# Two graph layers on one core: places of the edges by cumulative sums over block masks instead of rank products, a deeper split of the rows, and two more FP32 chunks

## The chip, the cores and the metric

The program runs on one core of a Trainium2 chip. A core has PE (TensorE, matrix products, with its weight loads shown as PEld), DVE (VectorE), ACT (ScalarE), POOL (GpSimd, which here issues the gathers) and SP (SyncE, which here issues most plain DMAs), each with an instruction queue of its own that runs in order. The metric is the device time of one execution in microseconds (us); lower is better.

## The reference: what is computed

There are N = 20000 nodes with 256 features each and E = 340000 edges. The edges come sorted by `dst`; every node has one edge to itself, and the others stand in both directions. Each edge has one of 8 types. Cut to what matters:

```python
def rgcn(x, W, self_w, b):                       # W: 8 x 256 x 256
    msg = einsum('ni,rio->rno', x, W)[edge_type, src]
    return segment_sum(msg, dst) + x @ self_w + b

# layer 0: two relational rounds, then residual and norm
h  = relu(rgcn(x, W1, self_w1, b1))
x  = layernorm(x + rgcn(h, W2, self_w2, b2))
# layer 1: attention with 4 heads of 64; here row = src, col = dst
h  = x @ W
e  = leaky_relu(hl[src] + hr[dst])               # hl, hr: sums of a_l * h, a_r * h by head
ee = exp(e - segment_max(e, src)[src])
out = segment_sum(ee / segment_sum(ee, src)[src] * h[dst], src)
return layernorm(x + out)
```

Layer 0 sums over `dst`, in which the edges are sorted. Layer 1 sums over `src`, in which they are not; so the kernel has to put the edges into an order by blocks of 128 source nodes before it can do the attention. That ordering is what the change is about.

## The kernel before

**Sizes.** P = 128. There are NB = 157 blocks of 128 nodes. The edges stand in COLS = 2657 columns of 128. A chunk is 16 columns (2048 edges, CH); there are NC = 166 chunks.

**Three stages.** Round one and round two (`rounds`, L756) are the two relational sums, each a pass of `by_chunks` (L588) over the 2657 columns. Then comes `attention` (L1301), block by block. Each stage gathers one 128-row tile per column with an indirect DMA from POOL: L607 in the rounds, L1354 in attention.

**A column in `by_chunks`.** POOL gathers 128 rows of the table at the columns' sources, AHEAD = 23 columns ahead, into one of 24 buffers `g`. PE multiplies them with a one-hot of destination and type (L727; the one-hots are made by DVE at L630, two of 1216 elements a chunk, or at L620 where rows are FP32) into PSUM tiles `a`. ACT and DVE evacuate these twice a chunk (L652, L650; the L650 copy closes a chunk), DVE adds the part carried over from the chunk before (L739), and `make` (L654) multiplies by the weights of the types (L662 to L674). `use` finishes the rows: in round one relu and a split in three BF16 parts (ACT L850, L854; DVE L852, L856), stored to the table `h2s` that round two gathers from.

**Rows as three BF16 parts.** The tables `xs` and `h2s` hold each row as three BF16 parts, so that PE can work in BF16 without losing FP32's digits. `xs` has to be made first: `split_rows` (L286) loads blocks of x, subtracts BF16 parts (ACT L301, L305; DVE L307, L312) and stores them with SP. Until then the first RAW = 26 chunks gather the FP32 rows of x themselves. When the gather of the first later chunk is put into the program, what is left of `split_rows` is drained before it (L603 to L605).

**Order by hand.** The pools' releases and the order of all instructions are as written (`manual_schedule`, L760): beside the chunks' own work, `by_chunks` takes side steps from a generator, at most one per column (L743): `pace(u)` says in which columns. In round one the side steps are the preparation of the edges (`heads`), then `split_rows` (two steps a block), then `order` (L795); round two goes on with `order`. In round one a step is taken in every column up to column 2 NB + COLS/3 + 120 and in five of six after that (L861); in round two in five of eight (L915).

**The ordering, class `ordered` (L918).** The columns are dealt to G = 29 groups: group g has the columns g, g + 29, and so on. `lots` are three columns of a group each. The steps:
- `count` (L994): a compare makes, for each lot, the one-hots of the block of each edge, `b16` (128 x 3 x 157; DVE L965), and one product a column (L1006) counts the edges by block.
- `records` (L970): seven passes of DVE over all 2657 columns pack what an edge has to carry into `hi` and `lo`.
- `places` (L1014): from the counts by group, where each group's edges of a block begin, within a record of 128 places; this also yields the list of the record rows.
- `write` (L1090): for each lot again the one-hots (L965), the rank of each edge among those of its block by two products a column (L1120, L1121), the place by a product with the one-hots and a maximum along the row (DVE L1141, L1144, L1145), a one-hot of the place `a16` (L1147), the one-hots scaled by `hi` and `lo` (`two`; ACT L1131, L1132, two a column), and one product a column (L1159) that sums a group's edges into records; `finish` (L1166) stores them. PSUM tiles `pr` and `pl` are used by all of this, one buffer each; `pending` keeps `use` off `pr` while a rank stands in it.
- `unpack` (L1255): after the rounds, 23 gathers (L1262) bring the records back in the order of blocks.

Of the kernel before, what the change touches and what calls it, by code (L numbers as in the profile page):

```python
# [34 lines left out]
F32 = mybir.dt.float32  # L35
# [12 lines left out]
P = 128  # L48
# [17 lines left out]
AHEAD = 23  # L66
# [8 lines left out]
def gnn_kernel(  # L75
# [39 lines left out]
    RAW = min(26, NC // 2)  # L115
# [11 lines left out]
    GT = min(P, NB * 19 // 32)  # L127
    G = -(-COLS // GT)
# [157 lines left out]
    def split_rows(sp):  # L286

        def load(i):
            v = sp.tile([P, D], F32, name="y", bufs=4)
            nc.sync.dma_start(v[:rows(i)], x[i * P:i * P + rows(i)])  # L290
            return v
# [4 lines left out]
        for i in range(NB + 1):  # L296
# [13 lines left out]
            if i < NB:  # L310
                left = sp.tile([P, D], F32, name="x1")
                nc.vector.tensor_sub(left[:m], v[:m], t[:m, 0])  # L312
                old = m, i, left, t
# [69 lines left out]
    def edges(k, keep, pool, ps, words):  # L383


        NQ = -(-COLS // P)
# [48 lines left out]
        k["kb"] = keep.tile([P, COLS], FP16, name="kb")  # L435
        k["idx"], k["code"] = [], []
# [16 lines left out]

        for s, (q, n) in enumerate(slices):
# [8 lines left out]
            k["idx"].append(idx)  # L463
            fs = number(fs, n, nc.vector.tensor_copy)
# [31 lines left out]
            if s + 1 < len(slices):  # L496
                x_, n_ = slices[s + 1]
                got[s + 1] = [flat(src, x_, n_, -P, nc.sync), flat(dst, x_, n_, -NP, nc.sync),
                              flat(etype, x_, n_, 0, nc.sync)]
# [18 lines left out]
            yield  # L518
            v = m * T
# [24 lines left out]
            if s + 1 < len(slices):  # L544
                got[s + 1].append(flat(dst, x_, n_, NP, nc.sync, 1))
# [3 lines left out]
            cl = pool.tile([P, CS], BF16, name="cl")  # L549
            yield from turned(same, q, n, cl)  # L550
            block = pool.tile([P, CS], F32, name="at").bitcast(I32)
            nc.vector.tensor_single_scalar(block[:, :w], lo, 7, op=ALU.arith_shift_right)
            nc.vector.scalar_tensor_tensor(k["kb"][:, c:c + w], cl[:, :w], 1024.0, block[:, :w],
                                           op0=ALU.mult, op1=ALU.add)
# [201 lines left out]
    def rounds(words):  # L756
        with tc.tile_pool(name="pi", bufs=1, space=PSUM) as cps, tc.tile_pool(name="rows", bufs=1) as keep, \
# [7 lines left out]
            pi = cps.tile([P, WIDE], F32, name="pi")  # L765
            nc.vector.tensor_copy(pi, wide_iota)
# [4 lines left out]
            parts = split_rows(sp)  # L771
# [23 lines left out]
    def order(ranks, ps, pi, words):  # L795
        with tc.tile_pool(name="order", bufs=2) as op:
            yield from ranks.run(op, ps, pi)
        ranks.over = True
        yield
        with tc.tile_pool(name="unpack", bufs=2) as up:  # L800
            yield from ranks.unpack(up, ps, *words)
# [23 lines left out]
    def round_one(k, pools, wp, first, parts, side, ranks):  # L825
# [21 lines left out]
        def use(j, p, _):  # L847
# [13 lines left out]
                  lambda u: u < 2 * NB + COLS // LOT + 120 or u % 6, False, ranks, RAW, parts)  # L861

    def round_two(k, pools, wp, side, ranks):
# [51 lines left out]
        by_chunks(h2s, AHEAD, k, pools, weights, load, use, side, lambda u: u % 8 < 5, True, ranks)  # L915


    class ordered:  # L918
# [6 lines left out]
        def __init__(self, keep, k):  # L925
# [8 lines left out]
            self.count_all = keep.tile([P, G, NB], FP16, name="count_all")  # L934
# [3 lines left out]
            self.band = keep.tile([P, 2 * P - 1], FP16, name="band")  # L938
            nc.vector.memset(self.band, 0.0)
            nc.vector.memset(self.band[:, P - 1:P], 1.0)  # L940
# [4 lines left out]
            self.below16 = keep.tile([P, P], FP16, name="below16")  # L945
            nc.vector.tensor_copy(self.below16, self.below)
# [10 lines left out]
            for g in range(G):  # L957
                n = len(range(g, COLS, G))
                self.lots += [(g, i, min(LOT, n - i), n) for i in range(0, n, LOT)]

        def blocks_of(self, sp, pi, lot):
            g, i, n, _ = lot
            b = sp.tile([P, LOT, NB], FP16, name="b16", bufs=4)
            c = g + G * i
            nc.vector.tensor_tensor(b[:, :n], pi[:, :NB].unsqueeze(1).to_broadcast([P, n, NB]),  # L965
                                    self.k["kb"][:, c:c + G * (n - 1) + 1:G].unsqueeze(2).to_broadcast([P, n, NB]),
# [21 lines left out]
        def run(self, sp, ps, pi):  # L988
            yield from self.count(sp, ps, pi)
            yield from self.records()  # L990
            yield from self.places(sp, ps)
            yield from self.write(sp, ps, pi)

        def count(self, sp, ps, pi):  # L994

            made = {m: self.blocks_of(sp, pi, self.lots[m]) for m in range(2)}
            pc, done = None, 0
            for m, (g, i, n, of) in enumerate(self.lots):
                if m + 2 < len(self.lots):
                    made[m + 2] = self.blocks_of(sp, pi, self.lots[m + 2])  # L1000
                b = made.pop(m)
                for x in range(n):
                    u = i + x
                    if u == 0:
                        pc = ps.tile([P, 512], F32, name=("pr", "pl")[g % 2])[:, :NB]
                    nc.tensor.matmul(pc, self.band[:, P - 1 - u:2 * P - 1 - u], b[:, x, :],  # L1006
                                     start=(u == 0), stop=(u == of - 1))
                    if u == of - 1:
                        nc.scalar.copy(self.count_all[:, g, :], pc)
                    done += 1  # L1010
                    if done % LOT == 0:
                        yield

        def places(self, sp, ps):  # L1014
# [3 lines left out]
            for g in range(G):  # L1018
                nc.tensor.matmul(pc, self.band[:, P - 1 - g:2 * P - 1 - g], self.count_all[:, g, :],
                                 start=(g == 0), stop=(g == G - 1))  # L1020
# [69 lines left out]
        def write(self, sp, ps, pi):  # L1090
# [7 lines left out]
            def begin(g):  # L1098


                x = ps.tile([P, 512], F32, name="pr")[:, :3 * NB].rearrange("p (a b) -> p a b", a=3)
                nc.tensor.matmul(x[:, 0, :], self.below16, self.count_all[:, g, :], start=True, stop=False)
                of = self.ident16[:, g:g + 1].to_broadcast([P, P])
                nc.tensor.matmul(x[:, 0, :], of, self.place16, start=False, stop=True)
                nc.tensor.matmul(x[:, 1, :], of, self.place16, start=True, stop=True)
                nc.tensor.matmul(x[:, 2, :], of, self.cross16, start=True, stop=True)
                start = sp.tile([P, NB], FP16, name="start")
                nc.scalar.copy(start, x[:, 0, :])
                cross = sp.tile([P, NB], F32, name="cross")
                nc.scalar.copy(cross, x[:, 2, :])  # L1110
                mine = sp.tile([P, NB], F32, name="mine")
                nc.vector.tensor_scalar(mine, x[:, 1, :], self.row, None, op0=ALU.is_le)
                group[g] = start, cross, mine

            def rank(m):
                g, i, n, _ = lots[m]
                pr = ps.tile([P, 512], F32, name="pr")[:, :LOT * NB].rearrange("p (x b) -> p x b", x=LOT)
                self.pending = True
                for x in range(n):
                    nc.tensor.matmul(pr[:, x, :], self.below16, made[m][:, x, :], start=True, stop=False)  # L1120
                    nc.tensor.matmul(pr[:, x, :], self.ident16[:, i + x:i + x + 1].to_broadcast([P, P]), group[g][0],  # L1121
                                     start=False, stop=True)
                ranked[m] = pr
# [806 lines left out]
```

## Time and profile before

| | |
|---|---|
| median of three runs | 10266.15 us (10256.0 to 10272.33) |
| profiled execution, its own time | 10269.47 us |
| its span | 10267.7 us |
| busy: PE, PEld | 8999.7 us (88%), 6985.1 us (68%) |
| busy: DVE, ACT | 7476.9 us (73%), 5836.7 us (57%) |
| busy: POOL | 7646.4 us (74%) |
| gathers from x and xs, from h2s, from table3s | 2657, 2657, 2657 |
| first gather of xs starts at | 607.39 us |
| first gather of h2s (round two) at | 3458.35 us |
| first gather for attention at | 6848.11 us |

How to read it: busy times are sums over the span, and stages differ. So the stretches matter more than the totals; POOL's busy time is the 0.95 us of each gather and leaves out what lies between two of them. In lists of instructions `out<-in` are the program's tile names with partitions x elements, `[0.30 <-PE a L727]` is the idle time before an instruction and what ended it. Line numbers are those of the kernel before.

### The profile page before, as it was taken

What the parts mean: (1) busy time and instruction counts of PE and PEld (TensorE: products, weight loads), DVE (VectorE), ACT (ScalarE), POOL (GpSimd) and SP (SyncE); (2) the same over time, 40 slices, a digit from 0 to 9 for tenths busy, and PEclk for the clock granted to TensorE, in tenths of its full rate; (3) what the DMA queues carried; (4) which work ended last, traced back from release to release, by engine and by line L of the source; (5) the groups of instructions that cost most, each with busy time, mean ns of one, the idle gap of its engine ahead of it and who ended that gap; (6) DMA issues with size and microseconds to landing.
All of it is one profiled execution on the core that took longest, in us unless ns stands there. A gap on an engine that the chain in (4) does not pass through costs nothing. (4 is left out here: it accounts for less than half of the span.)

```text
span 10267.7 us, 220891 instructions
## 1 busy us (share of the span) xinstructions
PE 8999.7 (88%) x75895; PEld 6985.1 (68%) x75895; DVE 7476.9 (73%) x21331; ACT 5836.7 (57%) x18175; POOL 7646.4 (74%) x8041
## 2 busy tenths in 40 slices
PE   7889999999999899999999999977777777777777
PEld 6778888888888788888888888854444444444444
DVE  5466667777777666666666666548888888888888
ACT  2321112555555544444444444438888888888888
POOL 7767777777777677777777777777777777777776
PEclk9999999999999999999999999989999999999999
DMA  5766666666666566666666666655555555555554
GB/s 176 233 185 179 179 178 174 179 179 177 179 178 178 171 188 189 187 187 189 186 188 187 184 186 185 186 164 156 154 154 153 155 154 154 155 154 153 155 155 129
DMA packets 860800, 1779.85 MB, mean 173 GB/s; under 512 B 196893, under 2 KB 525835, under 8 KB 859643
## 3 DMA queue, kind: packets, MB, share of 16 engines
q0 software_dynamic: 461712, 1386.83, 49.2%
q1 hardware_dynamic: 390098, 371.58, 11.6%
q8 instruction: 597, 9.78, 0.4%
q10 hardware_dynamic: 7848, 7.20, 0.2%
q14 instruction: 545, 4.46, 0.2%
HBM read 1632.08 MB, written 132.98 MB: 172 GB/s over the span
## 5 line engine op out<-in xcount | busy, mean ns | idle before, releaser
L1354 POOL DMA_INDIRECT g<-table3s,words x2657 | 2564.3, 965 | 812.7 <-issue 771.7
L607 POOL DMA_INDIRECT g<-h2s,idx x2657 | 2518.5, 948 | 873.2 <-issue 369.1
L674 PE MATMUL pm<-wt,to 128*128 128x256 f32 x10624 | 2894.5, 395 | 0.0
L727 PE MATMUL a<-s,g 128*128 128x152 bf16 (+8 forms) x34932 | 2793.8, 223 | 54.8 <-ACT xs L301 16.0
L607 POOL DMA_INDIRECT g<-xs,idx x2241 | 2134.2, 952 | 710.8 <-issue 277.8
L727 PEld LDWEIGHTS <-g 128*128 128x128 bf16 x33060 | 2127.5, 98 | 312.2 <-DMA g<-xs,idx 23.2
L1456 ACT ACTIVATE g<-g 128x64 f32<-128x64 f32 x8088 | 1993.0, 332 | 0.0
L674 PEld LDWEIGHTS pm<-wt,to 128*128 128x128 f32 x10624 | 1814.8, 191 | 179.7 <-issue 2.5
L1470 PE MATMUL po<-g,s 128*128 128x260 f32 x5314 | 1739.0, 418 | 106.4 <-DVE g L1462 78.8
L652 ACT COPY to<-a 128x512 f32<-128x512 f32 x996 | 546.3, 583 | 1948.9 <-PE a L727 1920.0
L1414 DVE CUSTOM_DVE_ANT_0 dump<-pr,pen 128x768 bf16<-128x768 f32 x1876 | 1621.5, 908 | 33.1 <-PE pr L1411 31.4
L1411 PE MATMUL pr<-hpt,pick 128*128 128x512 bf16 (+2 forms) x3752 | 937.3, 333 | 421.3 <-DVE top L1414 419.5
L1141 DVE CUSTOM_DVE_ANT_0 dump<-pr,b 128x157 f16<-128x157 f32 x2657 | 712.4, 320 | 777.8 <-PE pr L1121 768.0
L1131 ACT ACTIVATE two<-b,words 128x157 f16<-128x157 f16 x2657 | 1123.4, 423 | 182.3 <-DVE b L965 119.4
L965 DVE TENSOR_TENSOR b<-pi,kb 128x471 f16<-128x471 f32 (+1 forms) x1798 | 1104.5, 635 | 144.5 <-PE pr L1006 73.6
L1470 PEld LDWEIGHTS po<-g,s 128*128 128x128 f32 x5314 | 850.6, 197 | 467.7 <-ACT g L1447 83.6
L1132 ACT ACTIVATE two<-b,words 128x157 f16<-128x157 f16 x2657 | 1102.5, 415 | 0.0
L1411 PEld LDWEIGHTS <-pick 128*128 128x128 bf16 x3752 | 379.2, 101 | 920.0 <-issue 794.0
L630 DVE TENSOR_TENSOR s<-pi,code 128x1216 bf16<-128x1216 f32 (+1 forms) x614 | 866.8, 1412 | 0.0
L1159 PE MATMUL pl<-two,a 128*128 128x314 f16 x2657 | 508.0, 300 | 50.1 <-DVE a L1147 48.4
L1400 ACT CAST hpt<-pr 12x768 bf16<-12x768 f32 (+1 forms) x469 | 350.0, 747 | 341.2 <-PE pr L1398 341.1
L739 DVE TENSOR_TENSOR to<-to,to 128x192 f32<-128x192 f32 x330 | 119.0, 361 | 582.5 <-ACT to L652 582.2
(290 smaller groups left out, 10582.4 us busy)
## 6 DMA issues: line engine op xcount, KB each, us to landing
ob<-ownd SPq DMA_DIRECT2D x625, 128.0 KB
g<-h2s,idx POOLq DMA_INDIRECT x2657
g<-table3s,words POOLq DMA_INDIRECT x2657
y<-in_x SPq DMA_DIRECT2D x321, 128.0 KB
g<-xs,idx POOLq DMA_INDIRECT x2241
h2s<-h SPq DMA_DIRECT2D x166, 192.0 KB
own<-h2s SPq DMA_DIRECT2D x166, 192.0 KB
xs<-xs SPq DMA_DIRECT2D x156, 192.0 KB
```

Of the source, the lines that this page charges most:

```text
L607: nc.gpsimd.indirect_dma_start(out=g, out_offset=None, in_=of, in_offset=bass.IndirectOffsetOnAxis(ap=idx[u // CS][:, u % CS:u % CS + 1], ...
L630: nc.vector.tensor_tensor(s, pi[:, :w].unsqueeze(1).to_broadcast([P, e - f, w]), codes(c, e - f).unsqueeze(2).to_broadcast([P, e - f, w]), ...
L674: nc.tensor.matmul(p, to[:, i % 2, i // 2, :P], wt[:, i % 2, i // 2, :], start=False, stop=(i == 2 * R - 1))
L727: nc.tensor.matmul(a[h, q][:, b:e, :].rearrange("p n r -> p (n r)"), g[:, v * D + h * P:v * D + (h + 1) * P], s, start=((h, q) not in begu ...
L965: nc.vector.tensor_tensor(b[:, :n], pi[:, :NB].unsqueeze(1).to_broadcast([P, n, NB]), self.k["kb"][:, c:c + G * (n - 1) + 1:G].unsqueeze(2 ...
L1131: nc.scalar.activation(two[:, 0, :], made[m][:, x, :], AF.Copy, scale=k["hi"][:, c:c + 1])
L1132: nc.scalar.activation(two[:, 1, :], made[m][:, x, :], AF.Copy, scale=k["lo"][:, c:c + 1])
L1354: nc.gpsimd.indirect_dma_start(out=g[:, t, :], out_offset=None, in_=table3s, in_offset=bass.IndirectOffsetOnAxis(ap=to3[:, b, t:t + 1], ax ...
L1411: nc.tensor.matmul(pr[:, t:t + n, :], pick[:, h, :], k["hpt"][:, q + t:q + t + n, :], start=True, stop=True)
L1414: nc.vector.tensor_tensor_reduce(out=dump[:, :m, :].rearrange("p t e -> p (t e)"), in0=pr[:, :m, :].rearrange("p t e -> p (t e)"), in1=k[" ...
L1456: nc.scalar.activation(gh[:, h, :], gh[:, h, :], AF.Copy, scale=k["g"][:, t, D + h:D + h + 1])
L1470: nc.tensor.matmul(k["po"], k["s"][:, t, :] if t < n else ident, k["g"][:, t, :SR], start=(t == 0), stop=(t == n))
```

## The change

What it does, in four parts:
1. `split_rows` opens a pool of its own with four buffers for each tile (five for the loaded rows) instead of sharing the rounds' pool with two; RAW is 28 instead of 26.
2. The groups are made otherwise: column c belongs to row r = c mod 128, and a group is RG = 4 such rows, so G = 32. The block numbers of the edges are kept in a second layout, `kbflat` (128 x 21 x 128, BF16): partition r holds the edges of the columns r, r + 128, and so on, one after the other. `edges` builds it directly from the loaded sources (`block`, `to`) and turns it into `kb`; the loads of the second slice move behind the code of the first.
3. `count` and the ranking in `write` are gone. `rank` comes in their place: for each of the 157 blocks ACT makes a 0/1 mask of 2688 elements a partition in two passes (Square, then Relu, which also sums it); PE multiplies the sum with `below` (a product of one column); DVE makes a running sum over the mask in PSUM, started from that, in six pieces of at most 512, and after each a predicated copy puts it into `place` where the mask is 1. Each block has eleven steps. At the end three DVE passes over all places take them modulo 128, and PE and ACT turn them into `slots`.
4. `write` has two steps a lot instead of three, without the rank products and the reductions; the one-hot of the place compares with `slots`. In round one a side step is taken in every column, in round two in five of nine.

The core of the diff:

```diff
-    RAW = min(26, NC // 2)
+    RAW = min(28, NC // 2)
...
-    GT = min(P, NB * 19 // 32)
-    G = -(-COLS // GT)
+    RG = 4
+    G = P // RG
+    NQ = -(-COLS // P)
...
-    def split_rows(sp):
+    def split_rows():
+        with tc.tile_pool(name="split", bufs=4) as sp:
+            yield from split_in(sp)
...
-            v = sp.tile([P, D], F32, name="y", bufs=4)
+            v = sp.tile([P, D], F32, name="v", bufs=5)
...
-            cl = pool.tile([P, CS], BF16, name="cl")
-            yield from turned(same, q, n, cl)
-            block = pool.tile([P, CS], F32, name="at").bitcast(I32)
-            nc.vector.tensor_single_scalar(block[:, :w], lo, 7, op=ALU.arith_shift_right)
-            nc.vector.scalar_tensor_tensor(k["kb"][:, c:c + w], cl[:, :w], 1024.0, block[:, :w],
-                                           op0=ALU.mult, op1=ALU.add)
+            to = k["flat"][:, q:q + n]
+            nc.vector.scalar_tensor_tensor(to, same[:, :n], 1024.0, block[:, :n], op0=ALU.mult, op1=ALU.add)
+            yield from turned(to, q, n, k["kb"][:, c:c + w])
...
-            pi = cps.tile([P, WIDE], F32, name="pi")
+            pi = cps.tile([P, WIDE + 1], F32, name="pi")
...
+        with tc.tile_pool(name="rank", bufs=2) as op:
+            yield from ranks.rank(op, ps, pi[:, WIDE:])
...
-                  lambda u: u < 2 * NB + COLS // LOT + 120 or u % 6, False, ranks, RAW, parts)
+                  lambda u: True, False, ranks, RAW, parts)
...
-        by_chunks(h2s, AHEAD, k, pools, weights, load, use, side, lambda u: u % 8 < 5, True, ranks)
+        by_chunks(h2s, AHEAD, k, pools, weights, load, use, side, lambda u: u % 9 < 5, True, ranks)
...
+            for b in range(NB):
+                mask = sp.tile([P, NQ * P], BF16, name="mask")
+                nc.scalar.activation(mask, every, AF.Square, bias=wide_iota[:, b:b + 1], scale=-1.0)
+                yield
+                nc.scalar.activation(mask, mask, AF.Relu, bias=ones[:, 0:1], scale=-1.0,
+                                     accum_out=self.hist[:, b:b + 1])
+                yield
+                pb = ps.tile([P, 512], F32, name="pr")
+                nc.tensor.matmul(pb[:, 0:1], self.below, self.hist[:, b:b + 1], start=True, stop=True)
+                yield
+                nc.vector.tensor_single_scalar(less[:, b:b + 1], pb[:, 0:1], -1.0, op=ALU.add)
+                yield
+                at, old = less[:, b:b + 1], None
+                for i, (c, n) in enumerate(cuts):
+                    scan = ps.tile([P, 512], F32, name=("pl", "pr")[i % 2])[:, :n]
+                    nc.vector.tensor_tensor_scan(scan, mask[:, c:c + n], zero.to_broadcast([P, n]), at,
+                                                 op0=ALU.add, op1=ALU.add)
+                    at = scan[:, n - 1:n]
+                    if old:
+                        nc.vector.copy_predicated(*old)
+                    old = place[:, c:c + n], mask[:, c:c + n].bitcast(I16), scan
+                    yield
+                nc.vector.copy_predicated(*old)
+                yield
+            slots = flat.rearrange("p q r -> p (q r)").bitcast(FP16)[:, :COLS]
+            whole = sp.tile([P, NQ * P], F32, name="whole", bufs=1).bitcast(I32)
+            nc.vector.tensor_copy(whole, place)
+            yield
+            nc.vector.tensor_single_scalar(whole, whole, P - 1, op=ALU.bitwise_and)
+            yield
+            nc.vector.tensor_copy(place, whole)
...
             def place_of(m):
...
-                    nc.vector.tensor_tensor_reduce(out=dump, in0=pr[:, x, :], in1=made[m][:, x, :], scale=1.0,
-                                                   scalar=0.0, op0=ALU.mult, op1=ALU.max, accum_out=r[:, x:x + 1])
...
-                                        r[:, :n].unsqueeze(2).to_broadcast([P, n, P]), op=ALU.is_equal)
+                                        self.slots[:, c:c + P * (n - 1) + 1:P].unsqueeze(2).to_broadcast([P, n, P]),
+                                        op=ALU.is_equal)
...
-                    rank(m + 1)
                     place_of(m + 1)
```

## Prediction

> **What bounds the kernel now.** First I read the table of busy time in stretches of 200 us (columns: stretch, length, then busy us and instruction count of PE, PEld, VectorE, ScalarE, POOL, then granted clock, DMA share, GB/s):
>
> ```profile
> 200.00:400.00 200.00, 170.18 (x1028) 152.91 (x1027) 98.36 (x219) 77.67 (x200) 139.73 (x146) 0.96 0.77 231
> 1000.00:1200.00 200.00, 193.81 (x2020) 167.86 (x2019) 137.28 (x224) 30.07 (x67) 151.44 (x160) 1.00 0.62 178
> 4000.00:4200.00 200.00, 188.49 (x1849) 161.73 (x1849) 130.48 (x467) 96.95 (x279) 151.26 (x161) 1.00 0.67 188
> 8000.00:8200.00 200.00, 155.81 (x876) 89.79 (x875) 177.11 (x437) 170.67 (x582) 151.88 (x159) 0.96 0.57 155
> ```
>
> Look at POOL's count: about 160 gathers per 200 us in round one, round two and attention alike, though PE, VectorE and ScalarE are loaded quite differently. Only the first row (FP32 chunks) has fewer. The timeline of POOL says why, and where the exceptions are:
>
> ```profile
> 1203.94 0.94 POOL L607 DMA_INDIRECT g<-xs,idx  x1 [0.30 <-PE a L727]
> 1205.19 0.95 POOL L607 DMA_INDIRECT g<-xs,idx  x1 [0.30 <-PE pl L1006]
> ...
> 578.03 0.94 POOL L607 DMA_INDIRECT g<-in_x,idx  x1 [0.52 <-PE a L727]
> 607.39 1.10 POOL L607 DMA_INDIRECT g<-xs,idx  x1 [28.42 <-PE a L727]
> ...
> 3423.03 0.95 POOL L607 DMA_INDIRECT g<-xs,idx  x1 [0.30 <-issue]
> 3458.35 0.94 POOL L607 DMA_INDIRECT g<-h2s,idx  x1 [34.37 <-PE pl L1159]
> ```
>
> A gather takes 0.95 us and is followed by 0.30 us of idleness whatever the releaser named: one per 1.25 us. The page counts 3 x 2657 of them, and the unpacking adds 23: 7994 x 1.25 = 9993 us of the 10267.7 us span. The kernel is **bound by POOL issuing gathers**, and a change can win only what POOL waits beyond 0.30 us. Adding that up over POOL's timeline: 45 us before 580, 28.1 before the first gather of xs, 34.1 between the rounds, 29.6 between 4500 and 6600, 3.3 before attention: 140 us. Another 83 us are gathers longer than 0.95 us, 50 of them in attention, which is untouched.
>
> Next, how far PE is behind POOL: VectorE's L650 copy closes a chunk of 16 tiles; I take its start less the end of that chunk's last gather. It is 32 to 35 us in the FP32 chunks of the row splitting (chunk 16: 413.9 against 381.8), falls 0.45 us a chunk through the counting, is 5 us at chunk 107, 19.6 at the end of round one, 25 to 30 through the second half of round two, and falls 3 us a chunk once the writing is over there (6618.5, 6635.9, 6653.2: 17.2 us a chunk where POOL needs 20). With 24 gather buffers (30 us) POOL feels PE only where this distance is near 26 or more: in the FP32 chunks and in round two. So PE work removed elsewhere gives nothing by itself.
>
> **The change part by part** (against the profiled execution's 10269.5 us; the median shown is 3.3 us less).
>
> *Row splitting.* The waits between 200 and 560 (engine, line, what it waited for: us, times, longest):
>
> ```profile
> ACT xs L305 <- DMA xs<-xs: 136.8, 104, 2.9
> DVE x L312 <- ACT xs L305: 136.7, 113, 2.9
> PE pm L670 <- ACT ot L665: 37.7, 16, 3.7
> PE a L727 <- ACT xs L301: 16.0, 10, 2.3
> ```
>
> ScalarE stops 1.3 us a row for the store of the row before last, VectorE stops behind it, and PE then waits 53.7 of 360 us for copies queued behind that stop. The store waited for was issued one step (two tiles, 2.75 us) earlier, so it takes some 4.1 us; four buffers leave three steps, 7.5 us: the wait goes. A chunk here takes 22.0 us (288 gathers from 182.3 to 578.0: 1.374 us each), of which PE idles 53.7/360 x 22.0 = 3.3; 18.7 remain, under POOL's 20. So POOL is next, at 1.25: 288 x 0.124 = 35.7 us less. Then the 28.1 us: in the built program the first xs gather is placed at tile 416 - 23 = 393, when 13 rows are unsplit and are drained at once (L305 runs last at 603.1, the gather starts at 607.4). With 28 chunks it is placed at 425, and the splitting ends at 420, 6 us earlier, against 4.1 us of store. I leave 3 us of that gap. The two further FP32 chunks stay under POOL's pace (18.7 against 20). Sum: **-61**; bounds -64 (all) and 0 (the cover of the distance gone, the gap merely moved).
>
> *Counting becomes ranking*: 157 blocks of 11 steps, one step a tile, 13.75 us a block at POOL's pace. Removed: 2657 matmuls and 886 compares, hidden behind POOL: nothing. Added, per block:
> - ScalarE: two passes over 2688 elements. From L652 (512 wide: 0.58) and L665 (256 wide: 0.36), 2.5 us each, 5 us; its present work in round one is 30 of 200 us, 2.1 a block. 7.1 of 13.75: hidden.
> - PE: one matmul of one column. At 17.2 us a chunk, PE needs 11.8 us for 11 tiles: 1.9 us spare.
> - VectorE: six scans and six predicated copies (five of 512, one of 128). Neither is in the trace. Steps between starts, read where two instructions follow closely:
>
> ```profile
> 3422.90 1.41 DVE L630 TENSOR_TENSOR s<-pi,code 128x1216 bf16<-128x1216 f32 x1
> 3424.23 0.64 DVE L965 TENSOR_TENSOR b<-pi,kb 128x471 f16<-128x471 f32 x1
> ...
> 3442.28 0.68 DVE L650 COPY to<-a 128x512 f32<-128x512 f32 x1
> 3442.88 0.64 DVE L965 TENSOR_TENSOR b<-pi,kb 128x471 f16<-128x471 f32 x1
> ```
>
>   1216 elements: 1.33; 512: 0.60; so 1.04 ns an element, and 0.20 for 128. Lower bound 0.60, upper bound 1.33, for scan and copy each. VectorE's present work per chunk: 2 x 1.33 + 0.60 + 0.28 (L739) + 0.34 (L852) + 0.33 (L856) + 0.28 of idleness before L739 = 4.5, so 3.1 for 11 tiles. A block with both at 0.60: 5 x 1.20 + 0.40 + 0.35 (the small add and waits) + 3.1 = 9.9 us. Scan at 1.33: 13.5. Both at 1.33: 17.2. I take 0.60 for both, by L650, which has their width and reads PSUM; the first two sums stay under 13.75, so the forecast needs only the copy to be ordinary. **0**; bounds 0 and +534 ((17.2 - 13.75) x 157), of which the gathers ahead absorb some 25.
>
> [...] No run here shows a scan yet. [...]
>
> *Three passes over all places* (to integers, mask, back). The like passes of the records (L973 to L984, seven of them) stretch five gathers at 1697.8 to 1710.3 by 7.1 us together; three more: **+3** (0 to +7).
>
> *Writing.* Per lot of three columns the rank matmuls and reductions go; blocks, `two`, the transposed one-hots and three matmuls stay, in two steps. ScalarE's `two` starts every 0.32 us: 6 x 0.32 = 1.9 us a lot of 2.5 us in round one, plus 0.3 of its other work: 88%. PE: three matmuls step by 0.41 together (3439.54 to 3439.95), 8 lots a chunk: 3.3 us. The counting shows PE at 19.55 us a chunk with 48 matmuls of 0.067 in it: 16.3 without. 19.6 of 20. The distance should stay low: 8 us at the end of round one rather than 19.6, and the gap of 34 us shrinks by **-11** (0 to -15; 16 us of it are the last chunk's own chain). In round two, 16 x 5/9 / 2 = 4.4 lots a chunk: 17.2 + 4.4 x 0.41 = 19.0 of 20, so the distance falls instead of standing at 26, and the 29.6 us go: **-29** (0 to -30).
>
> Sum: -61 + 0 + 3 - 11 - 29 = **-98**: 10269.5 - 98 = 10171.5, some 10168 beside the median; I say **10170**. With the three waits gone as far as their bounds allow it would be 10160.
>
> **Rivals.**
> *A. VectorE becomes the bound* (the one that ends slower). The next block's small matmul on PE waits for the last predicated copy of this block, for their shared PSUM tile `pr`, and everything behind it on PE, the chunks' matmuls, waits too. From 1.98 us per 512-wide scan plus copy the block passes 13.75 us; each 0.1 us more costs 5 x 0.1 x 157 = 79 us; from 2.14 it eats the gain. At both upper bounds: 10171 + 534 - 25 = 10680; midway 10400. For it: neither price is known. Against: it needs both near the price of 1216 elements.
> *B. Not the throughput but the loop.* ScalarE's sum for a block stands one step before that matmul; if a pass sits behind an evacuation that waits for PE, PE waits for up to 5 us less three steps. A period of 14.2 instead of 13.75: 0.45 x 157 - 25 = +46: 10215. PE's spare 1.9 us speak against, VectorE's queue (scans between evacuations) for.
> *C. The FP32 stretch stays slow*, held by its transfers: the DMA engines are 77% busy at 1.374 us a gather and would be 85% at 1.25. Then only the 28 us go: 10207.
> *D. The change does not do what it says*: the distance at the end of round one stays, ScalarE at 88% in order being the late one: 10182, within the forecast's own range.
>
> **How the numbers follow.** Forecast with D 54% (10145 to 10190; its low end is that 10160 less the 16 us over which the runs shown spread), B 20% (10190 to 10250), C 10% (near 10207), A 16% (from 10250 up). The range 10145 to 10290 takes in the first three and the beginning of A. A measurement here tells about 0.2% (20 us) from no change. Faster: 54 + 10 + 17 of B = 81%; within: 3 of B and 3 of A = 6%; slower: 13%.
>
> **What would show it.** Right: POOL at 160 gathers per 200 us from 200 on; no gap over 5 us at the first xs gather; L305's wait for its store gone; VectorE 65 to 95% busy between about 550 and 2700, with the L650 distance falling there; a gap near 23 us between the rounds; none in round two. Wrong: under 158 gathers per 200 us in the ranking, with PE waiting for VectorE or ScalarE at the small matmul; scan plus copy over 1.98 us; POOL's gathers stretched beyond 0.95 us by the new VectorE work, which like L630 and L965 reads one operand from PSUM and which I therefore count at nothing.

## The result: slower by 4%, and where the time went

| | before | after |
|---|---|---|
| median of four runs each | 10268.83 us (10256.0 to 10272.33) | 10685.3 us (10681.54 to 10688.19) |
| ratio, 95% interval | | 1.0408 (1.039 to 1.0426) |
| profiled execution, its span | 10267.7 us | 10679.8 us |

10170 had been predicted, with 10145 to 10290 as the range. Lines of the kernel after carry other numbers than before: the gather is L618 (was L607), the copy that closes a chunk L661 (L650), a column's product L738 (L727). New are ACT's two passes L1016 and L1018, the one-column product L1022, DVE's running sum L1029 and its predicated copies L1033 and L1036.

POOL's gathers come in the same order in both kernels, so a gather's start in the one less its start in the other tells how much had been lost up to there:

| up to | after less before | of that in this stage | predicted |
|---|---|---|---|
| column 416 of round one, before's first gather of xs (splitting) | -55.0 us | -55 | -61 |
| column 2200 of round one (ranking, then whole passes and records) | +369.4 | **+424** | 0 and +3 |
| last column of round one (writing) | +408.4 | +39 | -11, with the next line |
| first gather of round two | +423.0 | +15 | |
| first gather for attention | +405.6 | -17 | -29 |
| end of the span | +412.1 | +7 | 0 |

The ranking alone loses as much as the whole kernel, and the splitting won nearly what was forecast. The busy time by stretches of the two kernels, before first (columns: stretch, its length, PE, PEld, DVE, ACT and POOL busy with their instructions, PE's granted clock, DMA share, GB/s):

```profile
200.00:400.00 200.00, 170.18 (x1028) 152.91 (x1027) 98.36 (x219) 77.67 (x200) 139.73 (x146) 0.96 0.77 231
800.00:1000.00 200.00, 192.71 (x2022) 167.13 (x2019) 138.24 (x224) 30.05 (x67) 151.27 (x161) 1.00 0.63 178
2000.00:2200.00 200.00, 189.08 (x1898) 160.04 (x1896) 145.53 (x512) 113.40 (x334) 151.52 (x160) 1.00 0.63 179
```

The same stretches of the kernel after:

```profile
200.00:400.00 200.00, 191.23 (x1192) 170.51 (x1192) 114.60 (x265) 89.79 (x242) 152.41 (x157) 1.00 0.85 266
800.00:1000.00 200.00, 154.31 (x1273) 129.75 (x1273) 158.18 (x205) 82.84 (x85) 123.82 (x132) 0.84 0.51 147
2000.00:2200.00 200.00, 152.22 (x1240) 128.63 (x1238) 159.53 (x207) 84.16 (x85) 125.80 (x133) 0.84 0.52 149
```

POOL's count is the pace. In the splitting it rises from 146 to 157 gathers per 200 us. In the ranking it falls from 160 to 132, and there **no engine is full**: between 800 and 1000 PE is 77% busy, DVE 79%, ACT 41%. What sets the pace is then not one engine's work but the waits between engines. POOL's timeline in the kernel after shows the places that had been looked at before:

```profile
552.35 0.95 POOL L618 DMA_INDIRECT g<-in_x,idx  x1 [0.30 <-issue]
...
592.85 0.95 POOL L618 DMA_INDIRECT g<-xs,idx  x1 [0.30 <-issue]
...
1446.02 0.95 POOL L618 DMA_INDIRECT g<-xs,idx  x1 [0.31 <-issue]
1450.55 0.95 POOL L618 DMA_INDIRECT g<-xs,idx  x1 [3.58 <-PE a L738]
...
3831.40 0.95 POOL L618 DMA_INDIRECT g<-xs,idx  x1 [0.42 <-PE a L738]
3881.31 0.95 POOL L618 DMA_INDIRECT g<-h2s,idx  x1 [48.96 <-PE pl L1178]
```

Before's 28.4 us of idleness ahead of column 416 are gone: the kernel after, with 28 FP32 chunks, still gathers from x there, at 552.35, and its first gather of xs, 32 columns later, follows its forerunner after 0.30 us. In the ranking POOL now waits up to several us at a time for PE. And the gap between the rounds grew from 34.4 to 49.0 us. What PE waits for between 800 and 2800 (engine, line, what it waited for: us, times, longest):

```profile
PE pr L1022 <- ACT mask L1018: 215.3, 53, 5.9
PE pr L1022 <- DVE place L1036: 154.9, 55, 6.5
PE pm L685 <- DVE to L661: 67.7, 17, 5.2
PE pr L1022 <- DVE to L661: 34.6, 7, 5.1
```

The busy time of these 2000 us, with the columns as above:

```profile
800.00:2800.00 2000.00, 1531.79 (x12790) 1291.98 (x12791) 1589.81 (x2065) 833.58 (x860) 1258.30 (x1327) 0.84 0.51 148
```

POOL issued 1327 gathers, so 120.6 blocks of eleven, each of 16.6 us instead of 13.8 (11 x 1.253, POOL's pace where nothing holds it: in the kernel before 639 gathers from 799.33 to 1598.75). PE was busy for 1531.8 us, 12.7 a block; it stood 3.4 us a block at the little product L1022 and 0.6 at L685: together 16.6, rounding aside, the whole block. One such ring, in the timeline of the kernel after:

```profile
1441.13 1.29 DVE L1029 TENSOR_TENSOR_SCAN pl<-mask,pr,pi 128x512 f32<-128x512 bf16 x1
1441.33 1.72 PE L738 MATMUL a<-s,g 128*128 128x144 bf16 x24
1441.53 0.39 ACT L866 ACTIVATE h<-pm 128x256 bf16<-128x256 f32 x1 [2.65 <-PE pm L685]
1442.34 0.72 DVE L1033 COPY_PREDICATED place<-mask,pr 128x512 f32<-128x512 int16 x1
1442.95 0.41 DVE L868 SCALAR_TENSOR_TENSOR left<-pm,h 128x256 f32<-128x256 f32 x1
...
1443.39 0.41 ACT L870 CAST h<-left 128x256 bf16<-128x256 f32 x1 [1.48 <-DVE left L868]
...
1443.71 2.53 ACT L1016 ACTIVATE mask<-kbflat,wide_iota 128x2688 bf16<-128x2688 bf16 x1
...
1446.27 2.54 ACT L1018 ACTIVATE mask<-mask,ones 128x2688 bf16<-128x2688 bf16 x1
1448.71 0.19 ACT L1018 ACTIVATION_READ_ACCUMULATOR mask<-mask,ones 128x1 f32 x1
1448.95 0.58 PE L1022 MATMUL pr<-hist,below 128*128 128x1 f32 x2 [5.90 <-ACT mask L1018]
```

ACT waits 2.65 us for PE's L685 and 1.48 for DVE's L868, which itself stands behind the scan and the predicated copy shown above it; only then do its two passes start, though the first of them reads neither result, and PE, having run out of work at 1443.05, waits for their end. Each engine has room, but each waits in its turn for another one's queue.

### The profile page after: what moved, and what is told of

The parts are those of the page before. It is cut to its first block, busy times and chain, and to the rows that moved or that the text cites. A ratio compares the mean times of both kernels' runs of the same rounds, so it can differ in the third digit from the quotient of the medians.

```text
span 10679.8 us, 199248 instructions
## 1 busy us (share of the span) xinstructions
PE 8845.1 (83%) x68106; PEld 6702.8 (63%) x68106; DVE 7499.6 (70%) x15385; ACT 6573.9 (62%) x18606; POOL 7671.9 (72%) x8044
## 4 chain that ended last, share of the span: by engine, by line
PE 42%; DVE 21%; ACT 14%; issue 9%; POOL 9%; DMA 4%; SPq 0%; ACTq 0%; DVEq 0%; POOLq 0%
PE pm L685 20%; PE a L738 12%; POOL g L1361 8%; DVE dump L1421 5%; PE pm L681 3%; DVE place L1033 3%; DVE pl L1029 2%; ACT g L1463 2%; DVE pr L1029 2%; PE pl L1178 2%; ACT two L1158 2%; ACT two L1159 2%; DMA g<-table3s,words 2%; ACT mask L1018 1%; PE pr L922 1%
## 5 line engine op out<-in xcount | busy, mean ns | idle before, releaser
L618 POOL DMA_INDIRECT g<-h2s,idx x2657 | 2525.3, 950 | 863.5 <-issue 375.9
L685 PE MATMUL pm<-wt,to 128*128 128x256 f32 x10624 | 2999.3, 406 | 88.3 <-DVE to L661 88.3
L738 PE MATMUL a<-s,g 128*128 128x152 bf16 (+9 forms) x34860 | 2913.0, 230 | 66.5 <-DMA g<-h2s,idx 31.2
L618 POOL DMA_INDIRECT g<-xs,idx x2209 | 2106.5, 954 | 1133.3 <-PE a L738 784.9
L738 PEld LDWEIGHTS <-g 128*128 128x128 bf16 x32844 | 2291.1, 102 | 486.2 <-issue 77.2
L685 PEld LDWEIGHTS pm<-wt,to 128*128 128x128 f32 x10624 | 1870.4, 197 | 292.0 <-DVE to L661 99.3
L641 DVE TENSOR_TENSOR s<-pi,code 128x1216 bf16<-128x1216 f32 x610 | 859.5, 1409 | 0.0
L1178 PE MATMUL pl<-two,a 128*128 128x314 f16 x2657 | 554.3, 302 | 126.7 <-DVE a L1165 75.9
L982 DVE TENSOR_TENSOR b<-pi,kb 128x471 f16<-128x471 f32 (+1 forms) x896 | 568.2, 634 | 1.3 <-ACT two L1159 1.3
L618 POOL DMA_INDIRECT g<-in_x,idx x448 | 443.9, 991 | 144.1 <-issue 75.0
```

The costliest lines, as they stand in the source:

```text
L618: nc.gpsimd.indirect_dma_start(out=g, out_offset=None, in_=of, in_offset=bass.IndirectOffsetOnAxis(ap=idx[u // CS][:, u % CS:u % CS + 1], ...
L641: nc.vector.tensor_tensor(s, pi[:, :w].unsqueeze(1).to_broadcast([P, e - f, w]), codes(c, e - f).unsqueeze(2).to_broadcast([P, e - f, w]), ...
L685: nc.tensor.matmul(p, to[:, i % 2, i // 2, :P], wt[:, i % 2, i // 2, :], start=False, stop=(i == 2 * R - 1))
L738: nc.tensor.matmul(a[h, q][:, b:e, :].rearrange("p n r -> p (n r)"), g[:, v * D + h * P:v * D + (h + 1) * P], s, start=((h, q) not in begu ...
L1178: nc.tensor.matmul(pl[0].rearrange("p a b -> p (a b)"), a[:, x, :], ranked.pop((m, x)).rearrange("p a b -> p (a b)"), start=(first and x = ...
```

## The experiments

Two theories. **Loop** (theory 1 in the expectations): PE stands at L1022 because ACT's sum and DVE's last copy of the block before come late in their queues; moving these away from the product cures it. **VectorE** (theory 2): a scan with its copy takes too long for eleven steps; only less work or more steps help. Times in the ranking are given for a block, from POOL's gathers between 800 and 2800. e2, e3, e6, f2 and g3 are one execution each; runs of one kernel spread over some 16 us.

**ACT's passes a block ahead (e2).** The two passes for block b + 1 are issued among the scans of block b; the block keeps eleven steps.

```diff
-                nc.scalar.activation(mask, every, AF.Square, ...)     # and Relu, each before a yield
+                mask = masks.pop(b)
...
+                    if b + 1 < NB and i == 1:
+                        squares(b + 1)
+                    if b + 1 < NB and i == 3:
+                        ones_of(b + 1)
...
+                yield
+                yield
```

> The changed kernel, with ScalarE's two passes for the next block put among this block's scans (eleven steps a block still), so that their sum is there long before PE's one-column product. Theory 1 (a loop: PE stands at that product, 3.4 us a block, 236 of 449 us for ScalarE and 173 for the last predicated copy): the ScalarE part goes, about 1.8 us of each of 157 blocks, so 10400 to 10450 instead of 10685; PE's idle time before the product falls to the copy's share. Theory 2 (VectorE is simply too slow: scan plus copy 1.96 us a cut): nothing changes, 10660 to 10690.

10387.8 us, 298 less than the kernel after and 12 below the range of theory 1; theory 2 had it unchanged. PE's waits between 800 and 2800 in this kernel, where the product is L1031 and the last copy L1049:

```profile
PE pr L1031 <- DVE place L1049: 213.6, 104, 5.3
PE pm L681 <- ACT ot L676: 145.2, 51, 3.8
```

The wait for ACT's sum is gone and the block takes 14.7 us instead of 16.6; 0.9 over POOL's pace remain, now with DVE named at the product and ACT at L681.

**The product in a place of its own (e3), and both (e4).** The one-column product writes a spare column of the tile `pi` instead of `pr`, so that DVE's last copy out of `pr` needn't be over.

```diff
-                pb = ps.tile([P, 512], F32, name="pr")
-                nc.tensor.matmul(pb[:, 0:1], self.below, ...)
+                pb = zero[:, 1:2]                                     # pi is one column wider
+                nc.tensor.matmul(pb, self.below, ...)
```

> The changed kernel, with the one-column product written to a free column beside the constants in PSUM instead of the tile pr that the scans use, so that it no longer waits for the last predicated copy. Theory 1 (loop): the wait for VectorE (173 us in 133 blocks, 1.3 us a block) goes, the one for ScalarE stays: 10480 to 10600. Theory 2 (VectorE too slow): 10660 to 10690, since the scans themselves are as long.

> Both edits together: passes one block ahead, and a PSUM column of its own. Theory 1 (loop): the ranking goes at POOL's pace, 13.8 us a block for 16.55; VectorE's 13.2 us of work still fit. The 424 us lost between gathers 480 and 2200 come back but for some 50: 10260 to 10320. Theory 2 (VectorE too slow): 10600 or more.

e3: 10681.7 us, no change. e4: 10390.4 us (four runs, ratio to before 1.0123, 1.0106 to 1.014), no better than e2 and in neither theory's range. PE's waits in e3 tell why:

```profile
PE pi L1022 <- ACT mask L1018: 214.0, 52, 5.9
PE pi L1022 <- DVE s L641: 186.3, 39, 7.8
```

The edit exchanged the wait for L1036 for one of the same size: DVE's L641 reads the same tile `pi`, and it is in the same queue. So e3 did not take the wait for DVE away. That its time lies in theory 2's range therefore says little; what e3 shows is that the product waits for DVE's *queue*, whichever of its instructions it is that it needs.

**Five of six predicated copies left out (e6).** The places are not made, so the edges' records and attention's lists of rows are not those of the reference.

```diff
-                    if old:
-                        nc.vector.copy_predicated(*old)
```

> The changed kernel without five of the six predicated copies of a block (only the last, of 128 places, is left; the places of the others stay zero, so the order of the edges is not made). VectorE has 3.3 us less to do in a block, 9.9 instead of 13.2. Theory 2 (VectorE too slow): POOL's pace, 10250 to 10290. Theory 1 (loop): PE's wait for VectorE goes, that for ScalarE stays or grows: 10450 to 10550.

11772.6 us, which neither theory foresaw. The trace puts the surplus behind the ranking: up to the first attention gather e6 is 261 us ahead of the kernel after (6992.9 against 7253.7), and then loses some 1350 in attention, whose gathers by these lists are slow (last section). So only the ranking is read: 14.95 us a block. PE's waits there:

```profile
PE pr L1022 <- ACT mask L1018: 318.8, 82, 5.3
PE pm L685 <- DVE to L661: 35.9, 17, 2.7
PE pr L1022 <- DVE place L1034: 11.0, 9, 1.3
```

DVE is now 68% busy (1365.5 of 2000 us) and PE's wait for its last copy is nearly gone, but the wait for ACT's sum is larger than in the kernel after. Each theory has half: taking either engine out of the way leaves 0.9 to 1.2 us a block.

**Both out of the way, and more steps instead of less work.** Two readings of what e2 still loses, V and P, stand in the expectations below. Four kernels: row splitting alone (e1, read below); passes ahead and five copies left out (e8); passes ahead and 13 steps a block (e9) or 12 (e10), by two idle `yield`s or one at the end of a block and a pace in round two of 5 in 8 or 3 in 5, since the writing starts later.

```diff
-                  lambda u: u % 9 < 5, True, ranks)
+                  lambda u: u % 8 < 5, True, ranks)
...
                 nc.vector.copy_predicated(*old)
                 yield
                 yield
                 yield
+                yield
+                yield
```

> The kernel before with the first part of the change alone: row splitting with four buffers of its own and 28 FP32 chunks; the ranking by matrix products stays. If the 55 us that the changed kernel was ahead at its first gather of xs are this part's, and are kept to the end because nothing after them has changed: 10205 to 10225 us. If they are given back at the end of round one or in round two, where the distance between POOL and PE is largest, 10255 to 10270.

> The kernel with ScalarE's two passes moved a block ahead, and five of the six predicated copies of a block left out as well, so that the places are not made and nodes get wrong slots; the attention stage then fetches the same rows again and again, so only the time up to the first attention gather is read (6848 us before, 7254 after, 6968 with the passes ahead alone). Theory V, that what is left of the loss in the ranking is VectorE's queue (13.0 us of work in a block of 13.75): the ranking runs at 157 to 160 gathers per 200 us and the first attention gather comes at 6790 to 6830. Theory P, that PE alone, at the granted clock of 0.89 it has there, takes 1.33 us a tile: 150 gathers per 200 us and 6950 to 6970, as with the passes ahead alone.

> The passes ahead, and 13 steps to a block in place of 11 (16.25 us at POOL's pace); the writing then begins 317 tiles later and runs in round two at 5 steps of 8 in place of 5 of 9. Theory V: VectorE has 13.6 us of work in 16.25 us, the ranking runs at 158 to 160 gathers per 200 us, the distance falls in it and the gap between the rounds is near 30 us: 10205 to 10250 us. Theory P: 150 gathers per 200 us over more tiles, 10380 to 10430.

> The same with 12 steps to a block (15.0 us at POOL's pace) and 3 steps of 5 in round two. Theory V: VectorE has 13.3 us of work in 15.0; the ranking runs at 155 to 160 gathers per 200 us: 10210 to 10300 us. Theory P: 150 gathers per 200 us, 10380 to 10420.

Beside these four the kernel before itself took 14124.57 us (e1 14080.05, e8 13829.57, e9 13870.04, e10 13811.71 us; ratios to before 0.9967, 0.9954 to 0.9979, for e1 and 0.9813, 0.9797 to 0.983, for e9). Why all of them took so long was not tried; they can't be set beside the runs above, and the kernels were run again beside a kernel before of some 10270 us.

> The passes ahead, 13 steps to a block (16.25 us at POOL's pace), 5 steps of 8 in round two; the same kernel as e9, beside a kernel before of some 10267 us. Theory V (VectorE's queue, 13.6 us of work in 16.25): 158 to 160 gathers per 200 us in the ranking, 10205 to 10250 us. Theory P (PE alone needs 1.33 us a tile at the granted clock of 0.89): 150 gathers per 200 us, 10380 to 10430.

> The passes ahead, and five of the six predicated copies of a block left out; the places are not made, so only the time up to the first attention gather is read (6848 us before, 7254 after, 6968 with the passes ahead alone). Theory V: 157 to 160 gathers per 200 us in the ranking, first attention gather at 6790 to 6830. Theory P: 150 per 200 us, 6950 to 6970.

f1: 10259.2 us (ratio 0.9996, 0.9986 to 1.0005), 9 over the range of theory V. f2: first attention gather at 6815.7 us, as theory V had it. The ranking in f1, by stretches as above:

```profile
800.00:1000.00 200.00, 173.39 (x1531) 143.09 (x1530) 165.27 (x216) 87.40 (x98) 151.26 (x161) 0.91 0.62 178
1800.00:2000.00 200.00, 171.13 (x1530) 140.54 (x1528) 171.53 (x226) 88.69 (x99) 151.55 (x160) 0.93 0.62 178
```

And in f2, from 800 to 2600 in one:

```profile
800.00:2600.00 1800.00, 1547.18 (x13836) 1278.44 (x13834) 1324.60 (x1582) 896.83 (x929) 1362.35 (x1438) 0.92 0.63 178
```

160 gathers per 200 us in both: POOL is the bound again, and the ranking is as theory V had it; what f1 loses beyond that lies after it, at the gap between the rounds (47.4 us) and in round two. f2 reaches POOL's pace with eleven steps at a granted clock of 0.92. In e2, at 0.89, PE was not the bound either:

```profile
800.00:2800.00 2000.00, 1641.20 (x14377) 1368.66 (x14375) 1787.68 (x2327) 930.00 (x965) 1420.68 (x1498) 0.89 0.58 167
```

1641 us for 1498 tiles are 1.10 us a tile, not 1.33: theory P falls.

**Is more slack alone enough, and how much is needed?** g3 is the kernel after with 13 steps and 5 in 8, ACT's passes left in place; g2 is e10 again.

> The changed kernel with 13 steps to a block and 5 of 8 in round two, but ScalarE's two passes left where they are, a step and two ahead of the small product. If slack for VectorE is the whole cure: 158 to 160 gathers per 200 us in the ranking and 10245 to 10275 us, as with the passes ahead and 13 steps (10259). If the order of the loop costs by itself, PE standing at the small product for ScalarE's sum whatever the budget: PE's waits there stay near 1.5 to 2 us a block and the ranking at 135 to 152 gathers per 200 us, 10350 to 10600.

> The passes ahead, 12 steps to a block (15.0 us at POOL's pace) and 3 steps of 5 in round two, as in e10. If VectorE's work alone counts (13.3 us of 15.0, 89%): 158 to 160 gathers per 200 us in the ranking, as with 13 steps, and less distance to pay for in round two than 5 of 8 cost (the first 30 us): 10225 to 10255 us. If waits of the loop still come on top at 89%: 152 to 157 gathers per 200 us and 10270 to 10350.

g3: 10493.73 us, 17.7 us a block of 13, 1.4 over POOL's pace. Its PE waits between 800 and 2800:

```profile
PE pr L1022 <- ACT mask L1018: 287.9, 71, 5.3
PE pm L685 <- DVE to L661: 129.6, 35, 5.2
PE pr L1022 <- DVE place L1036: 6.8, 14, 0.5
```

The wait for DVE's last copy has gone with the slack, the one for ACT has not (2.5 us a block), and the one at L685 has grown. g3 and f1 differ only in where ACT's passes stand, so the order costs by itself. g2: 10250.53 us (ratio 0.9977, 0.9967 to 0.9986), as expected if VectorE's work alone counts; its ranking and PE's longest wait for another engine there:

```profile
800.00:2800.00 2000.00, 1714.35 (x15337) 1408.12 (x15336) 1782.47 (x2324) 927.16 (x996) 1513.88 (x1595) 0.93 0.62 178
```

```profile
PE pr L1031 <- DVE place L1049: 50.5, 36, 2.1
```

With DVE busy 13.4 of 15.0 us the ranking costs nothing. All variants of the ranking together; the budget is the steps times 1.253, times are for a block:

| kernel | ACT's passes | budget | DVE busy | block | over the budget |
|---|---|---|---|---|---|
| after | in place | 13.8 us | 13.2 us | 16.6 us | 2.8 us |
| e3, own column | in place | 13.8 | 13.2 | 16.7 | 2.9 |
| e6, five copies out | in place | 13.8 | 10.2 | 14.95 | 1.2 |
| g3, 13 steps | in place | 16.3 | 13.8 | 17.7 | 1.4 |
| e2 | a block ahead | 13.8 | 13.1 | 14.7 | 0.9 |
| e4, own column | a block ahead | 13.8 | 13.1 | 14.8 | 1.0 |
| f2, five copies out | a block ahead | 13.8 | 10.1 | 13.8 | 0 |
| g2, 12 steps | a block ahead | 15.0 | 13.4 | 15.05 | 0 |
| f1, 13 steps | a block ahead | 16.3 | 13.7 | 16.3 | 0 |

With DVE at 74% of the budget (e6) or 85% (g3) ACT in place costs 1.2 to 1.4 us a block. A DVE at 95% costs 0.9 with ACT's passes ahead (e2), and the two together 2.8, more than their sum.

**Row splitting alone (g1).** The kernel before, with only part 1 of the change.

```diff
-    RAW = min(26, NC // 2)
+    RAW = min(28, NC // 2)
...
+        with tc.tile_pool(name="split", bufs=4) as sp:
+            yield from split_in(sp)
```

> Row splitting alone, as in e1, beside a kernel before of some 10267 us. If its 55 us are kept to the end: 10205 to 10225 us. If they are given back at the end of round one or in round two: 10255 to 10270.

**10203.3 us**, ratio 0.9932 (0.9915 to 0.9949): the fastest of all, faster than both kernels, and 2 below the range in which the 55 us are kept. It is 60 us ahead of before at column 416 and 70 to 75 from the middle of round two on. Its POOL timeline between the rounds (the gather is L611 there):

```profile
3364.22 0.95 POOL L611 DMA_INDIRECT g<-xs,idx  x1 [0.30 <-PE a L731]
3390.99 0.95 POOL L611 DMA_INDIRECT g<-h2s,idx  x1 [25.82 <-PE pl L1163]
```

The gap is 25.8 us where the kernel before has 34.4. PE is nearer to POOL there: the copy that closes the last full chunk of round one starts 10.2 us after that chunk's last gather, in before 19.6. The ordering's writing begins 28 columns later than in before; whether that is the reason was not tried.

This run bears on the rest of the change too. In g2 the new ranking costs nothing, yet g2 is 47 us slower than g1. Up to column 2200 the two are nearly level (64.7 and 58.9 us ahead of before); at the first gather of round two g2 is 33.0 ahead and g1 67.4, at the first attention gather 21.9 and 74.8. From column 2200 on, in the writing, at the gap and in round two, g2 thus loses 43 us against before, where the prediction had the new writing win 40. Which of the writing's steps costs this was not tried.

## Why the prediction was wrong

**What bounds the kernel, and the row splitting: right.** POOL at 1.253 us a gather is the bound wherever nothing holds it, in g1, f1 and f2 as in before. -61 was said, -55 came (-60 in g1). The wait for the store did go. The first waits of the kernel after between 200 and 560:

```profile
ACT xs L310 <- DMA v<-in_x: 66.8, 45, 3.0
DVE rest L317 <- ACT xs L310: 61.8, 39, 2.9
ACT xs L306 <- DVE rest L317: 58.3, 94, 1.1
```

In its place ACT waits for the load `v`, half as long, and PE is not among those that wait longest. Rival C, that transfers would hold the stretch, falls: 157 gathers per 200 us with the DMA engines at 85%, as the first row of the kernel after shows.

**Ranking at nothing: wrong, and the bulk of the miss.** The step that failed is *"the first two sums stay under 13.75, so the forecast needs only the copy to be ordinary"*. It failed twice.

First in a price: 0.60 us was taken for scan and copy each. DVE's timeline in the kernel after, where they follow each other:

```profile
1431.35 1.29 DVE L1029 TENSOR_TENSOR_SCAN pr<-mask,pl,pi 128x512 f32<-128x512 bf16 x1
1432.55 0.72 DVE L1033 COPY_PREDICATED place<-mask,pl 128x512 f32<-128x512 int16 x1
1433.31 1.29 DVE L1029 TENSOR_TENSOR_SCAN pl<-mask,pr,pi 128x512 f32<-128x512 bf16 x1
1434.51 0.72 DVE L1033 COPY_PREDICATED place<-mask,pr 128x512 f32<-128x512 int16 x1
```

The scan steps by 1.20, the copy by 0.76: 1.96 a pair instead of 1.20. The copy was near the ordinary price; the scan was near the other bound (1.33). DVE has 13.2 us a block, not 9.9.

From 128 to 512 elements the scan grows from 491 to 1291 ns (last section): 2.08 ns an element, twice the 1.04 that the prediction read off plain instructions.

Second, in the reasoning: even 13.2 is under 13.8, and the pair under the threshold of 1.98 at which rival A was to begin. By the prediction's own sum the measured prices give 13.8 (5 x 1.96 + 0.58 for the pair of 128 + 0.35 + 3.1), so a loss near nothing; 2.8 us a block came, 424 us. And e6, in which DVE has 10.2 us a block, close to the 9.9 that had been counted, still loses 1.2. A sum of busy time below the budget only says that an engine is not the bound by itself. Here the chain L685, L866, L868, L870, the two passes, L1022 and back goes round PE, ACT and DVE in each block, through queues that are almost full on one of them. e2 against f2 shows what remains of DVE's 95% when ACT is out of the way (0.9), e6 and g3 what ACT's place costs when DVE has room (1.2, 1.4).

**Rival B named the mechanism** (PE at the small product, ACT's pass behind an evacuation that waits for PE) and priced it at 0.45 us a block. The sign that it had named came: 132 gathers per 200 us, with PE waiting for VectorE and ScalarE at that product. "PE's spare 1.9 us speak against": that was taken from PE at a granted clock of 1.00 (before, 6600 to 6660), 1.075 us a tile. In the ranking PE takes 1.154 a tile (1531.8 us for 1327) at a granted clock of 0.84, so 0.9 of the 1.9 were gone. In e2 it is 1.096 at 0.89, in f1 1.077 at 0.92; how much of this is the clock was not separated.

The mean granted clock between 800 and 2800 was 1.00 in the kernel before, where PE's longest wait for another engine is 4.2 us, 0.84 in the kernel after, where it is 6.5, and 0.93 in g2, where no wait of PE's exceeds 3.2. Whether the waits have to do with the clock was not tried.

**Whole passes +3: right.** Longer gathers around the passes add up to 9.8 us, against 7.1 in before; in the ranking a gather stays at 0.95 us (1258.3 for 1327).

**Writing in round one -11: wrong**, +39 and +15 came. PE's busy time was well forecast (19.3 us a chunk against 19.6), but the chunk takes 21.4 and POOL 149 gathers per 200 us. PE's waits from 3200 to 3850 in the kernel after:

```profile
PE pl L1178 <- DVE a L1165: 27.5, 53, 2.4
PE pr L1211 <- DVE here L1200: 20.3, 8, 3.6
```

The same error again: the sum holds, the waits between engines come on top. The kernel after pays all of it at once, since the ranking leaves PE 35 us behind POOL. In f1 the distance is 8 us when the writing begins and 27 at its end; POOL keeps its pace to the end of round one, and only the gap between the rounds (47.4 us) stays.

**Round two -29:** -17, the right sign. At 5 in 9 it loses 10 us against POOL's pace up to its last gather; f1, at 5 in 8, gives back 34 us between its first and the first attention gather.

**Rival A** (10400 to 10680) had nearly the right total for a reason that is half of it: VectorE is late, but not past its budget.

## What to carry to other kernels

A busy sum under the pace shows that an engine isn't the bound by itself, not that the work is hidden. Where a unit of work goes round several engines within one period, each hop can wait for what happens to stand ahead in an engine's queue (in the ring shown, ACT 2.65 and 1.48 us and PE 5.90). What cured it here was both to issue the producer a whole period ahead and to leave the fullest engine some 10% (89% cost nothing, 95% cost 0.9 us a block); either alone was not enough. And a change of several parts deserves to be taken apart: the first part alone was the fastest kernel here.

## What the runs showed of the hardware that was not expected

- The running sum, by form, and the copy between 800 and 2800 of the kernel after (mean ns last before the bar):

```profile
L1029 DVE TENSOR_TENSOR_SCAN pl<-mask,pr,pi 128x512 f32<-128x512 bf16 x241 | 311.1, 1291 | 5.9
L1033 DVE COPY_PREDICATED place<-mask,pl 128x512 f32<-128x512 int16 x362 | 261.8, 723 | 0.0
...
L1029 DVE TENSOR_TENSOR_SCAN pr<-mask,pl,pi 128x128 f32<-128x128 bf16 x120 | 58.9, 491 | 2.9
```

- A sum that ACT makes along with a pass costs an instruction of its own, 0.19 us (L1018, in the timeline above).
- In e6, attention's gathers, whose lists of rows were broken because the places had not been made, take the DMA engines 2.5 times as long as whole lists. From 8000 to 8400 us the packets of the queue of the gathers take 73.4% of the time of 16 engines there, for 227 gathers, which is 20.7 us of one engine each; in the kernel after it is 40.8% for 315, 8.3 us each. Which rows they hit was not looked at.
